# A causal latent-attention block with its query and key operands held as pairs of fp16 in place of pairs of rounded fp32

## The chip, the cores and the metric

The kernel runs on one core of a Trainium2 chip. A core has a matrix engine (TensorE, PE in the profile, with its weight loads as PEld), VectorE (DVE), ScalarE (ACT), GpSimd (POOL) and SyncE (SP), which mainly issues DMAs. The engines run side by side, each serves its own instructions in order, and they wait for one another by semaphores. TensorE writes to the accumulators in PSUM; ACT and DVE read them there. The metric is the time of one execution on the device in microseconds; lower is better.

## The reference

The input x has 2048 rows of 512 numbers, in fp32. One attention layer with compressed queries and keys is followed by a linear layer, each with a residual sum and a layer norm:

```python
cq = rms_norm(x @ w_qa.T, q_a_ln_w)                    # 2048 x 384
q = (cq @ w_qb.T).reshape(1, 2048, 16, 192)            # 16 heads: 128 plain + 64 rotary
ckv = x @ w_kva.T                                      # 2048 x (128 + 64)
ckv_l = rms_norm(ckv[..., :128], kv_a_ln_w)
k_nope, v = split((ckv_l @ w_kvb.T).reshape(1, 2048, 16, 256), 128)
# q_pe, k_pe: rotary parts; k_pe is one for all heads
scores = (q_nope @ k_nope.T + q_pe @ k_pe.T) * 192 ** -0.5, causal mask
out = softmax(scores) @ v, heads joined, @ w_o.T
x = layernorm(x + out)
x = layernorm(x + x @ (weight * scale_weight[:, None]).T + bias)
```

## The kernel before

**Numbers.** TensorE takes rounded fp32 (F32R) or fp16. To keep accuracy, an operand is held as a pair: a high part h, the value in the narrower type, and a low part l, the value less h. A product of two pairs takes three matmuls, hh, hl and lh. `split` (L61 to L68) makes a pair: one ACT instruction (L64, or L67 with a scale) writes h, one DVE instruction (L65 or L68) writes l. Before the change, softmax weights and values are pairs of fp16 (L495, L498; V), and the query latents, query weights, queries, keys and rotary parts are pairs of F32R.

**Heads.** The key up-projection is folded into the query weights: `weights_q` (L139) multiplies, for each of four groups of four heads, the plain query weights by the key weights (L170) and splits the result; so all heads share one key of 128 numbers, `Kn`, and one rotary key, `Kp`. In `score` (L409 to L427) a tile of scores takes five matmuls (L421): three with the plain query `qn` and `Kn`, two with `pe` and `Kp`. Of `pe`'s 128 partitions 64 hold the rotary query's high part and 64 its low part, while `Kp` holds the key twice. The causal mask is added on the diagonal tile, by a small matmul (L423) or by DVE (L427).

**Setup and side work.** x is worked through in eight half blocks of 256 rows. `project_x` (L198) computes keys for 128 rows at a time, with x stationary (L221), then the query latents already transposed, 3 x 12 matmuls of 256 columns with the weights stationary (L251). Keys are normalised with `rsqrt` on POOL (L195, L196), transposed by TensorE (L268, L269) and split. The latents are not normalised: `query_norms` computes 1/rms for each row (L283, L288) into `rq`, which enters as the scale of the softmax. Latents and weights that are not needed at once go to DRAM (`cq_d`, `wq_d`, `wpe_d`), and `load_block`, `load_wq`, `load_wpe` fetch them again for each query block. Half blocks 0 and 1 and weight group 0 come first, in setup; the rest is side work between the steps of query block 0.

**Query blocks.** Four blocks of 512 rows; in each, `units` (L627) goes through eight pairs of heads and four tiles of 128 rows. Per head and tile: scores, row maximum (DVE L459), exp with row sum (ACT L474; in block 0, L515 and L521), normalised weights as a pair (ACT L495, DVE L498), a transposing DMA on SP's queue, and the product with the values (`values`, L551), a few tiles later. `project_nope` (L391) and `project_pe` (L347) make the queries of the next pair between the score tiles; POOL forms `pe` (L359, L360, L373, L374). A score tile has its row of 128 queries against all keys up to the diagonal, cut into chunks of at most 512 columns (`chunks`, L35): 320 to 512 columns in block 1, up to four chunks in block 3.

**Order.** In setup and block 0 a scheduler orders each engine's instructions by a timeline of its own, with four PSUM buffers tagged `m` for all small products. From block 1 on TensorE's and SP's order is the program's, and from block 3 also that of ACT and DVE. In block 3 three PSUM buffers take turns for score tiles of up to 1024 columns, two of them for each head. After block 3 the output stage applies w_o and the linear layer with pairs of F32R (L770, L880).

## Time and profile before

| | us |
|---|---|
| median of 3 runs | 1588.42 (1587.66 to 1588.46) |
| profiled execution, its span | 1586.4 |
| setup, to the first score matmul | 36.66 |
| block 0 | 212.09 |
| block 1 | 242.85 |
| block 2 | 356.10 |
| block 3 | 476.80 |
| output stage | 261.90 |

The boundaries are the starts of the first score matmul of each block. In lines of groups, the name of the tile written stands left of the arrow, the tiles read right of it, then partitions x elements and the type, xcount, busy time and mean duration of one in ns, and the idle time of the engine just before them. In a line of the timeline the first number is the start, the second the time from the first start to the last end of the merged instructions. A matmul's duration includes filling and draining, which overlap with its neighbours', so that starts, not durations, tell its cost.

### The profile page before, as it was taken

The numbers are of one execution on the slowest core, as the hardware profiler recorded it, in microseconds if no ns is written. First come the engines' busy times: TensorE is split into PE (matmuls) and PEld (weight loads), VectorE is DVE, ScalarE is ACT, GpSimd is POOL, SyncE is SP. The second block draws the span as 40 slices with busy tenths as digits, with TensorE's granted clock in tenths as the row PEclk, the third lists the DMA queues.
The fourth block names the chain that finished last, engine by engine and source line by source line (L and its number), as shares of the span: only waits on it lengthen the run. The fifth ranks groups of instructions, "written<-read, shape, count | busy, mean of one in ns | idle before, by whom it ended". The sixth has DMA issues, their size and how long they took to land. (4 is left out here: it accounts for less than half of the span.)

```text
span 1586.4 us, 24671 instructions
## 1 busy us (share of the span) xinstructions
PE 1546.3 (97%) x9130; PEld 1291.1 (81%) x9130; DVE 1161.2 (73%) x2099; ACT 924.7 (58%) x1631; POOL 361.5 (23%) x434
## 2 busy tenths in 40 slices
PE   8899998999999999999999999999999999999997
PEld 7688877888887788888888788888888886788886
DVE  6777777878787978787786877877777775465564
ACT  5767776665665676666765665665666665311120
POOL 2243325154016204050032401400400000022132
PEclk9999999999999999999999999999999999999999
DMA  7879877788897987788897888878678798433230
GB/s 230 258 197 240 191 191 160 147 176 190 149 218 163 173 163 165 159 162 170 160 204 148 168 145 168 156 143 165 140 143 176 148 233 196 146 118 122 94 113 33
DMA packets 633032, 262.49 MB, mean 165 GB/s; under 512 B 570288, under 2 KB 611376, under 8 KB 631888
## 3 DMA queue, kind: packets, MB, share of 16 engines
q1 hardware_dynamic: 621472, 233.62, 68.8%
q0 software_dynamic: 4672, 17.73, 3.6%
q10 hardware_dynamic: 6768, 9.57, 2.1%
q8 instruction: 72, 1.18, 0.3%
q14 instruction: 48, 0.39, 0.1%
HBM read 83.17 MB, written 35.13 MB: 75 GB/s over the span
## 5 line engine op out<-in xcount | busy, mean ns | idle before, releaser
L421 PE MATMUL s<-Kn,qn 128*128 128x512 f32 (+4 forms) x1920 | 521.1, 376 | 9.4 <-ACT pr L474 4.4
L474 ACT ACTIVATE pr<-s,bias,rq 128x1024 f32<-128x1024 f32 (+3 forms) x320 | 324.4, 1017 | 217.0 <-DVE bias L468 157.2
L498 DVE SCALAR_TENSOR_TENSOR hl<-pr,inv,hl 128x1024 f16<-128x1024 f32 (+7 forms) x320 | 359.6, 1137 | 38.7 <-ACT hl L495 34.9
L421 PEld LDWEIGHTS s<-Kn,qn 128*128 128x128 f32 x1920 | 339.5, 190 | 55.7 <-ACT pr L474 7.4
L551 PEld LDWEIGHTS <-V 128*128 128x128 f16 x3264 | 302.5, 98 | 86.6 <-issue 47.6
L551 PE MATMUL o<-ring,V 128*128 128x256 f16 x3024 | 362.9, 273 | 2.5 <-DVE qn L68 1.2
L421 PE MATMUL s<-Kp,pe 128*128 128x512 f32 (+4 forms) x1280 | 361.4, 363 | 0.0
L495 ACT ACTIVATE hl<-pr,inv 128x1024 f16<-128x1024 f32 (+7 forms) x320 | 294.6, 961 | 91.3 <-issue 34.5
L459 DVE TENSOR_REDUCE neg<-s 128x1 f32<-128x1024 f32 (+3 forms) x320 | 317.8, 993 | 38.0 <-PE s L421 34.9
L421 PEld LDWEIGHTS s<-Kp,pe 128*128 128x128 f32 x1280 | 234.0, 189 | 29.6
L359 POOL TENSOR_TENSOR prod<-prod 128x512 f32<-128x512 f32 x15 | 19.4, 1292 | 639.1 <-DVE prod L352 639.0
L391 PE MATMUL ps_qn<-cq,wq 128*128 128x512 f32 x576 | 145.1, 397 | 3.1 <-ACT ot L556 1.7
L770 PE MATMUL acc<-wvo,oh 128*128 128x512 f32 x448 | 143.9, 402 | 1.8 <-ACT pr L474 1.8
L374 POOL TENSOR_TENSOR pe<-prod,ph 32x512 fp32r<-32x512 f32 x92 | 138.8, 1509 | 6.0
L391 PEld LDWEIGHTS ps_qn<-cq,wq 128*128 128x128 f32 x576 | 107.3, 190 | 24.8 <-ACT ot L556 2.4
L770 PEld LDWEIGHTS acc<-wvo,oh 128*128 128x128 f32 x448 | 83.1, 188 | 23.2 <-issue 3.8
L486 DVE TENSOR_SCALAR inv<-sums 128x1 f32<-128x1 f32 x128 | 27.0, 211 | 97.5 <-ACT pr L474 97.5
L770 PE MATMUL acc<-wvo,ol 128*128 128x512 f32 x224 | 88.1, 393 | 0.0
L556 ACT ACTIVATE ot<-o 128x256 f32<-128x256 f32 x128 | 48.4, 378 | 45.2 <-PE o L551 39.6
L347 PE MATMUL ps_pe<-cq,wpe 128*128 128x512 f32 x288 | 73.8, 402 | 0.2 <-DMA cq<-cq_d 0.2
L64 ACT ACTIVATE oh<-o 128x1024 fp32r<-128x1024 f32 x28 | 29.7, 1060 | 65.6 <-PE acc L770 50.0
L65 DVE TENSOR_TENSOR ol<-o,oh 128x1024 fp32r<-128x1024 f32 x28 | 38.8, 1387 | 39.3 <-ACT oh L64 39.3
(147 smaller groups left out, 1631.6 us busy)
## 6 DMA issues: line engine op xcount, KB each, us to landing
wq<-wq_d SPq DMA_DIRECT2D x22, 768.0 KB, 5.7
o<-ot_d SPq DMA_DIRECT2D x32, 512.0 KB, 3.3
ot_d<-ot SPq DMA_DIRECT2D x97, 128.0 KB, 2.4
wpe<-wpe_d SPq DMA_DIRECT2D x10, 768.0 KB, 5.4
wq<-wq_d POOLq DMA_DIRECT2D x9, 768.0 KB, 6.4
cq_d<-cqst SPq DMA_DIRECT2D x18, 256.0 KB, 4.8
wo<-in_wo_dram SPq DMA_DIRECT2D x4, 1024.0 KB, 5.3
x<-in_x_dram SPq DMA_DIRECT2D x16, 256.0 KB, 3.7
```

Source lines behind the costliest of these rows:

```text
L65: nc.vector.tensor_tensor(l, ps, h.bitcast(F32), ALU.subtract)
L347: nc.tensor.matmul(ps, w[:, i, lt, x * P : (x + 1) * P], cq[:, k, lt, :], start=n == 0, stop=n == 8)
L374: (nc.gpsimd if not quick or (b, g) == (0, 0) and j % 2 else nc.vector).tensor_tensor(pe[64 + 32 * x : 96 + 32 * x, j, :], rp[q, x, :], ph ...
L391: nc.tensor.matmul(ps, w[:, i, lt, j * P : (j + 1) * P], cq[:, k, lt, :], start=n == 0, stop=n == 8)
L421: nc.tensor.matmul(ps[:, :w], lhs, K[:, i, c0 : c0 + w], start=n == 0, stop=n == 4)
L459: nc.vector.tensor_reduce(neg[:, ti : ti + 1], v, axis=AX.XY, op=ALU.max, negate=True)
L474: nc.scalar.activation(pr[:, c0 : c0 + n * w].rearrange("p (a c) -> p a c", a=n), v, AF.Exp, bias=bias, scale=r, accum_out=sums[:, ti : ti ...
L495: nc.scalar.activation(hl[:, 0, c], pr[:, c], AF.Copy, scale=inv)
L498: nc.vector.scalar_tensor_tensor(hl[:, 1, c], pr[:, c], inv, hl[:, 0, c], ALU.mult, ALU.subtract)
L551: nc.tensor.matmul(ps[:, :256], vt[:, i, k % 4, :], v[:, :, l, k, :], start=n == 0, stop=n == 3 * kts - 1)
L556: nc.scalar.activation(ot, ps[:, :256], AF.Copy)
L770: nc.tensor.matmul(acc, l[:, t, c], state["wvo"][p][:, i, j, :], start=p == 0 and j == 0 and n == 0, stop=p == NPAIR - 1 and j == 1 and n ...
```

## The change

Query latents, query weights, plain queries and plain keys become pairs of fp16. `split16` makes them, always with a scale, since fp16 has a narrow range. The scales come from norms computed on chip: `weights_q` first forms the sum of squares of a whole group (ACT Square with a running sum, a matmul with ones, a DVE sum, a root on POOL) and splits its products, now copied to SBUF, only then; `first_scales` takes a norm of `kvln` in setup. The latents are now normalised before they are stored: `project_x` computes 128 rows at a time with x stationary (12 matmuls of 384 columns), squares and scales them, transposes them by TensorE and splits them. The score scale is then one number for a group of heads (`er`) instead of one for a row.

The rotary parts stay F32R in block 0, with a key tile of its own (`Kp0`), and are fp16 from block 1 on. The scale of the rotary key needs all 2048 rows: `project_x` keeps it in fp32 (`Kr`) with sums of squares, and behind the last half block `late_keys` forms the scales and splits it into `Kp`. From block 1 on the rotary tables `cs` are multiplied on POOL by one of those scales when they are loaded.

Tiles, loads and stores of these operands have half the bytes; the two halves of a weight group lie apart in DRAM. The instructions of TensorE for fp16 are a weight load and a matmul each, for F32R one that does both. Input layout and output stage are unchanged.

```diff
+K_UP = 1024.0
+C_UP = 1024.0
+W_TOP = 32768.0
+C_TOP = 20100.0
+TINY = 1.0e-30
...
+    def split16(src, h, l, scale):
+
+        nc.scalar.activation(h, src, AF.Copy, scale=scale)
+        nc.vector.scalar_tensor_tensor(l, src, scale, h, ALU.mult, ALU.subtract)
...
-    cq_d = [dram.tile([P, 2, LT, QB], F32R, name=f"cq_d{b}") for b in range(NB)]
-    wq_d = [dram.tile([P, 2, LT, 512], F32R, name=f"wq_d{g}") for g in range(4)]
-    wpe_d = [dram.tile([P, 2, LT, 256], F32R, name=f"wpe_d{g}") for g in range(4)]
+    cq_d = [dram.tile([P, 2, LT, QB], F16, name=f"cq_d{b}") for b in range(NB)]
+    wq_d = [dram.tile([P, 2, 2, LT, 256], F16, name=f"wq_d{g}") for g in range(4)]
+    wpe_d = [dram.tile([P, 2, LT, 256], F16, name=f"wpe_d{g}") for g in range(4)]
...
+    def root(dst, src, n=1):
+
+        t = small.tile([P, 4], F32, tag="rs", name="rt_t")
+        nc.gpsimd.tensor_scalar_add(t[:, :n], src, TINY)
+        nc.gpsimd.tensor_tensor(dst, t[:, :n], half, ALU.pow)
...
+    def column_total(dst, sums, n):
+
+        ps = psum["m"].tile([P, 512], F32, tag="m", name="ps_tot")
+        nc.tensor.matmul(ps[:, :n], ones, sums, start=True, stop=True)
+        nc.vector.tensor_reduce(dst, ps[:, :n], axis=AX.X, op=ALU.add)
...
+        tot = small.tile([P, 1], F32, tag="tot", name="tot")
+        column_total(tot, sq, 1)
+        root(kvn, tot)
+        nc.vector.tensor_scalar(kvn, kvn, C_TOP, None, ALU.mult)
+        k0 = small.tile([P, 1], F32, tag="k0", name="k0")
+        nc.vector.reciprocal(k0, kvn)
+        nc.vector.tensor_scalar(kvq[0], kvln, k0, None, ALU.mult)
+        nc.vector.tensor_scalar(ku, k0, K_UP, None, ALU.mult)
...
+        column_total(tot, ksum, S // P)
+        fk = small.tile([P, 1], F32, tag="fk", name="fk")
+        root(fk, tot)
+        z = small.tile([P, 1], F32, tag="z", name="z")
+        nc.vector.scalar_tensor_tensor(z, fk, K_UP, kvn, ALU.mult, ALU.add)
+        k1 = small.tile([P, 1], F32, tag="k0", name="k1")
+        nc.vector.reciprocal(k1, z)
+        nc.vector.tensor_scalar(kvq[1], kvln, k1, None, ALU.mult)
+        nc.vector.tensor_scalar(up, k1, fk, K_UP / W_TOP, ALU.mult, ALU.mult)
+        nc.vector.tensor_scalar(er[1], fg, z, SM_SCALE / (W_TOP * C_UP * K_UP), ALU.mult, ALU.mult)
+        nc.vector.reciprocal(ks, fk)
+        nc.vector.tensor_scalar(ks, ks, W_TOP, None, ALU.mult)
...
     def weights_q(g, direct=None):
...
-            split(raw, to[:, 0], to[:, 1], sc)
-            move(nc.sync, wpe_d[g][:, :, lt], to)
+            nc.scalar.activation(
+                junk[:, :256], rpe[:, lt], AF.Square, scale=sc, accum_out=sums[:, LT + lt : LT + lt + 1]
+            )
+        wr = pa.tile([P, LT, 512], F32, tag="wr", name=f"wr{g}")
...
             ps = psum["m"].tile([P, 512], F32, tag="m", name=f"ps_wq{g}_{lt}")
             for j in range(4):
                 nc.tensor.matmul(ps[:, j * P : (j + 1) * P], raw[:, j, :], wk[:, j, :], start=True, stop=True)
+            nc.scalar.activation(junk, ps, AF.Square, scale=sc, accum_out=sums[:, lt : lt + 1])
+            nc.vector.tensor_copy(wr[:, lt], ps)
+            if lt < LT - 1:
+                yield
+        tot = small.tile([P, 1], F32, tag="tot", name="tot")
+        column_total(tot, sums, 2 * LT)
+        root(fg[:, g : g + 1], tot)
+        nc.vector.tensor_scalar(
+            er[0][:, g : g + 1], fg[:, g : g + 1], kvn, SM_SCALE / (W_TOP * C_UP * K_UP), ALU.mult, ALU.mult
+        )
+        rf = small.tile([P, 1], F32, tag="rf", name="rf")
+        nc.vector.reciprocal(rf, fg[:, g : g + 1])
+        qa = small.tile([P, LT], F32, tag="qa", name="qa", bufs=2)
+        nc.vector.tensor_scalar(qa, qln, rf, W_TOP, ALU.mult, ALU.mult)
+        st = Kp.rearrange("p a c -> p (a c)")[:, : 4 * LT * 256].rearrange("p (b a l c) -> p b a l c", b=2, a=2, l=LT)
+        to = direct[0] if direct is not None else st[:, 0]
+        for lt in range(LT):
+            sc = qa[:, lt : lt + 1]
+                split16(
+                    wr[:, lt].rearrange("p (a c) -> p a c", a=2), st[:, :, 0, lt], st[:, :, 1, lt], sc
+                )
             else:
...
+                split16(wr[:, lt, :256], to[:, 0, lt], to[:, 1, lt], sc)
+        pt = direct[1] if direct is not None else pa.tile([P, 2, LT, 256], F16, tag="wpst", name=f"wpst{g}")
+        for lt in range(LT):
+            split16(rpe[:, lt], pt[:, 0, lt], pt[:, 1, lt], qa[:, lt : lt + 1])
...
+            nc.sync.dma_start(wq_d[g], st)
+        nc.sync.dma_start(wpe_d[g], pt)
+        yield
...
     def project_x(hb, wkv, wqa, direct=None, raws=None):
...
+            nc.scalar.activation(junk[:, :P], ps[:, :P], AF.Square, scale=P ** -0.5, accum_out=ms[:, 0:1])
...
+            nc.scalar.activation(
+                junk[:, :64], kp[:, 0, :], AF.Square, accum_out=ksum[:, 2 * hb + i : 2 * hb + i + 1]
+            )
+            pc = psum["m"].tile([P, 512], F32, tag="m", name=f"ps_cq{hb}_{i}")
+            n = 0
+            for kt in range(KT):
+                for x_, w_ in ((xh, wqa[0]), (xh, wqa[1]), (xl, wqa[0])):
+                    nc.tensor.matmul(pc[:, : LT * P], x_[:, kt, cols], w_[:, kt, :], start=n == 0, stop=n == 11)
+                    n += 1
+            nc.scalar.activation(
+                junk[:, : LT * P], pc[:, : LT * P], AF.Square, scale=(LT * P) ** -0.5, accum_out=ms[:, 1:2]
+            )
+            rk = small.tile([P, 2], F32, tag="rk", name="rk")
+            rsqrt(rk, ms, 2, 1e-6)
+            nk = pa2.tile([P, P], F32, tag="nk", name="nk")
+            nc.vector.tensor_scalar(nk, ps[:, :P], rk[:, 0:1], None, ALU.mult)
+            nq = pa2.tile([P, LT * P], F32, tag="nq", name="nq")
+            nc.scalar.activation(nq, pc[:, : LT * P], AF.Copy, scale=rk[:, 1:2])
...
-            if i:
-                query_norms()
...
-            nc.scalar.activation(sq, ps[:, :256], AF.Square, scale=(LT * P) ** -0.5)
-            if lt:
-                nc.vector.tensor_tensor(acc, acc, sq, ALU.add)
...
+            pq = psum["m"].tile([P, LT, P], F32, tag="m", name=f"ps_qt{hb}_{i}")
+            for lt in range(LT):
+                nc.tensor.transpose(pq[:, lt, :], nq[:, lt * P : (lt + 1) * P], ident)
+            to = slice(o + i * P, o + (i + 1) * P) if direct is not None else cols
+            split16(pq, st[:, 0, :, to], st[:, 1, :, to], C_UP)
             yield
-        norms.append((hb, acc))
...
+        split16(pt[:, 0].rearrange("p a c -> p (a c)"), Kn[:, 0, cols], Kn[:, 1, cols], K_UP)
+        kf = pt[:, 1].rearrange("p a c -> p (a c)")
+        nc.scalar.activation(Kr[:, cols], kf, AF.Copy)
+        if hb < 2:
+            split(kf, Kp0[:, 0, cols], Kp0[:, 1, cols], ku)
+            nc.sync.dma_start(cq_d[b][:, :, :, half_of], st)
...
+    def late_keys():
+        late_scales()
+        yield
+        for c in range(0, S, 512):
+            split16(Kr[:, c : c + 512], Kp[:, 0, c : c + 512], Kp[:, 1, c : c + 512], ks)
+            yield
...
     def load_block(b):
...
-        cq = prj.tile([P, 2, LT, QB], F32R, tag="cq", name=f"cq{b}")
+        cq = prj.tile([P, 2, LT, QB], F16, tag="cq", name=f"cq{b}")
         if b:
-            move(state["queue"], cq, cq_d[b])
+            state["queue"].dma_start(cq, cq_d[b])
         cs = prj.tile([P, 2, QB], F32, tag="cs", name=f"cs{b}")
         (state["queue"] if b else nc.sync).dma_start(cs, a["csq"][b])
+        if b:
+            nc.gpsimd.tensor_scalar(cs, cs, up, None, ALU.mult)
...
+        w = state["wq", b, p] = prj.tile([P, 2, LT, 256], F16, tag="wq", name=f"wq{b}_{p}")
+        state["queue"].dma_start(w, wq_d[p // 2][:, p % 2])
...
+        w = state["wpe", b, g] = prj.tile([P, 2, LT, 256], F16, tag="wpe", name=f"wpe{b}_{g}")
+        state["queue"].dma_start(w, wpe_d[g])
...
+        kind = F16 if b else F32R
+        ph = prj.tile([P, 2, QB], kind, tag="ph", name=f"ph{b}_{g}")
         nc.scalar.activation(ph, rp, AF.Copy)
-        pe = blk.tile([P, 4, QB], F32R, tag="pe", name=f"pe{b}_{g}")
+        pe = blk.tile([P, 4, QB], kind, tag="pe", name=f"pe{b}_{g}")
...
+        qn = blk.tile([P, 2, 2, QB], F16, tag="qn", name=f"qn{b}_{p}")
...
-            split(ps, qn[:, 0, j, :], qn[:, 1, j, :], kvln)
+            split16(ps, qn[:, 0, j, :], qn[:, 1, j, :], kvq[1 if b else 0])
...
-        ops = [(qh, Kn, 0), (qh, Kn, 1), (ql, Kn, 0), (qp, Kp, 0), (qp, Kp, 1)]
+        kp = Kp if b else Kp0
+        ops = [(qh, Kn, 0), (qh, Kn, 1), (ql, Kn, 0), (qp, kp, 0), (qp, kp, 1)]
         n = 0
         for lhs, K, i in ops:
             nc.tensor.matmul(ps[:, :w], lhs, K[:, i, c0 : c0 + w], start=n == 0, stop=n == 4)
...
     def head_scores(pools, b, p, j, qt, nk, prev):
-        t = 4 * b + qt
-        r = rq[:, t : t + 1]
+        r = er[1][:, p // 2 : p // 2 + 1]
```

## Prediction

> **What bounds the kernel now.** I read the page first, then the busy time by stage, then the groups by form, then the timeline of TensorE, then the waits. The page says who is busy.
>
> ```profile
> span 1586.4 us, 24671 instructions
> PE 1546.3 (97%) x9130; PEld 1291.1 (81%) x9130; DVE 1161.2 (73%) x2099; ACT 924.7 (58%) x1631; POOL 361.5 (23%) x434
> ```
>
> The median of the runs is 1588.42 us, 2.0 above this execution's span; I add that 2.0 to every sum. The smallest change that a measurement of this kernel can tell from none is about 0.2%, 3.2 us.
>
> The windows cut the span at the first score matmul of each query block: setup, blocks 0 to 3, output stage. Columns: stretch, its length, busy time of PE, PEld, DVE, ACT, POOL, then granted clock, DMA share, GB/s.
>
> ```profile
> 0.00:36.66 36.66, 32.45 (x206) 27.30 (x207) 21.84 (x55) 20.88 (x54) 10.96 (x30) 1.00 0.69 224
> 36.66:248.75 212.09, 197.78 (x1309) 170.18 (x1308) 160.01 (x374) 153.30 (x392) 69.69 (x123) 0.98 0.85 216
> 248.75:491.60 242.85, 238.66 (x1432) 202.23 (x1429) 197.06 (x416) 151.51 (x242) 82.73 (x74) 0.99 0.85 175
> 491.60:847.70 356.10, 353.45 (x2149) 298.10 (x2149) 291.52 (x546) 240.15 (x432) 83.16 (x72) 1.00 0.84 167
> 847.70:1324.50 476.80, 473.54 (x2893) 393.08 (x2891) 355.70 (x511) 301.91 (x442) 65.10 (x56) 1.00 0.80 158
> ```
>
> Blocks 1 to 3 are TensorE from end to end; DVE is next, at 75 to 82%. In their 1075.8 us TensorE's listed waits sum to 10 us. So there a cheaper matmul is a shorter kernel. What a matmul costs is not its duration (pipelined, they overlap) but the distance between starts:
>
> ```profile
> 1299.25 2.13 PE L551 MATMUL o<-ring,V 128*128 128x256 f16 x18
> 1301.13 0.94 PE L421 MATMUL s<-Kn,qn 128*128 128x512 f32 x3
> 1301.91 0.63 PE L421 MATMUL s<-Kp,pe 128*128 128x512 f32 x2
> 1302.38 0.86 PE L421 MATMUL s<-Kn,qn 128*128 128x512 f32 x3
> ...
> 1303.55 0.77 PE L421 MATMUL s<-Kn,qn 128*128 128x448 f32 x3
> ```
>
> Five fp32 matmuls of 512 columns fill 1302.38 to 1303.55: 234 ns each. Over the trace the median distances at L421 are 234, 201, 176, 147, 118 ns for 512, 448, 384, 320, 256 columns, 230 at L391, 228 at L347. The fp16 ones of 256 columns (L551; above, 17 distances in 2.13 us less the last one's 0.27) stand 109 apart. The only fp16 matmuls of 512 columns are the ten warm-ups, whose closest starts are 216 apart. 109 and 216 give 0.418 ns a column plus 2, so fp16 should cost 216, 189, 162.5, 136, 109: from 9 ns (256) to 18 ns (512) less.
>
> **What the change takes from TensorE.** Block 1 has 160 score matmuls of each of 320, 384, 448, 512 columns, 144 of L391, 72 of L347: 160 x (11 + 13.5 + 12 + 18) + 144 x 14 + 72 x 12 = 11.6 us. Block 2: 80 x 9 + 320 x 13.5 + 560 x 18 + 144 x 14 + 72 x 12 = 18.0. Block 3: 160 x 36.5 + 800 x 18 + 126 x 14 + 54 x 12 = 22.6. Together **52.2 us**. Setup and block 0 have 162 of L391, 90 of L347 and three of five score matmuls (rotary pairs stay fp32 there): 3.4 + 96 x 9 + 48 x 13.5 + 48 x 18, together 5.7.
>
> The order of TensorE's instructions in blocks 1 to 3 is unchanged, and of ACT's and DVE's nearly so. What follows close behind: DVE's 197, 291.5 and 355.7 us stand in stretches of some 231, 338 and 454, which is 85, 86 and 78%. The tightest wait is in block 3, where the second score tile of a head reuses the buffer that an exp (L474) frees: in the trace that exp ended 0.88 us before (median), in 10 of 63 cases under 0.6; a head's first tile gets 0.15 to 0.18 us shorter. I charge **+3** for waits that appear, bounds 0 and +26 (half of the gain). The halved loads of weights and latents (768 KB in 5.7 us, 22 on SP) are hidden, and stay so; their cover is a pair's work of over 30 us.
>
> POOL's splits of the rotary part (1.29 us each, cast 0.76) now read and write fp16, which no row shows: from 0 to twice as long, 36 us for a group instead of 18. A group's users start over 40 us later, so nothing; without that cover up to 18 us a group, 11 groups. Block loads gain a POOL multiplication of the tables, 128x1024, by a row of 1.29 us for 128x512 some 2.6 us; SP issues the loads far ahead in blocks 2 and 3. In block 1 it stands before the latents' load in POOL's queue and waits for the new scales; users come some 11 us later, about what it all takes. Nothing, up to +5.
>
> **Setup: new round trips.** Now each 128 rows of latents are normalised before the transpose, and TensorE's order puts the three transposes right behind the twelve matmuls that they depend on, in setup with nothing between. One trip: Square 128x384 from PSUM 0.52 (row of 128x384, L64), accumulator read 0.19, POOL add 0.23 and pow 0.76 (128x2 rows of L195, L196), scaling on ACT 0.52, three hand-offs of 0.1: 2.5 us. Four trips: **+10.0**. On ACT the next half's split (2 x 0.63) stands ahead of the first Square and 0.5 ahead of the last scaling: **+1.7**. The weights now wait for their norm:
>
> ```profile
> 24.91 3.07 PE L170 MATMUL ps_wq<-wk,wqb_r 128*128 128x128 f32 x24
> 27.81 0.50 PE L283 MATMUL ps_rq<-ones,acc 128*128 128x1 f32 x4
> ```
>
> Today L391 starts at 28.42, 0.6 us behind L170. Then ACT has about 3.4 us of splits and Squares left (three of 0.69 + 0.19, four smaller of some 0.4, one in progress), and the chain total, sum, add and pow, three small DVE steps, first split adds 0.25 + 0.3 + 1.0 + 0.7 + 0.5, together 6.2 (I take 6.3): **+5.7**. So long an idle time also slows what follows, as one of today shows:
>
> ```profile
> 43.68 1.13 PE L170 MATMUL ps_wq<-wk,wqb 128*128 128x128 f32 x8 [4.10 <-DMA wqb<-in_wqb_dram]
> 44.57 5.95 PE L391 MATMUL ps_qn<-cq,wq 128*128 128x512 f32 x18
> ```
>
> The same 18 matmuls took 4.33 us from 28.42 on, 1.6 less. The windows around the waits show the clock (columns as above):
>
> ```profile
> 42.00:49.50 7.50, 5.82 (x23) 4.86 (x24) 4.24 (x6) 7.35 (x13) 1.88 (x3) 0.77 1.04 387
> 62.50:69.50 7.00, 4.62 (x24) 3.81 (x23) 5.15 (x17) 6.22 (x16) 0.00 (x0) 0.76 0.97 265
> 130.00:138.00 8.00, 6.04 (x27) 4.86 (x26) 5.72 (x14) 6.16 (x19) 1.08 (x2) 0.79 1.11 342
> 245.00:255.00 10.00, 5.93 (x26) 5.10 (x25) 8.84 (x14) 5.48 (x11) 2.29 (x4) 0.74 0.56 156
> ```
>
> They hold TensorE's waits of 4.10, 2.38, 1.96 and 2.68 us, and behind each the clock was halved for 3.4 us (6.8 behind the last); behind waits up to 1.75 us it was not. The new wait for the norm is one more: **+1.6**. The trips of 2.5 us stand among the rows that slow: 4 x 1.6 = **+6.4**, bound 0. The Trainium skill, in "TensorE: Matmul & The Clock Gate", section "What's actually happening", names at least one idle window of about 3.4 us as what halves the clock. By it trips of 2.5 us would cost nothing further, and the sum would be 1564; the rows of 1.96 to 2.68 us disagree, and I go by them.
>
> Projection itself: 24 x 176 + 6 x 109 for 36 x 120 ns per half block, +0.55; eight times +4.4, less 32 norm matmuls of about 0.1, −3.2: **+1.2** in all.
>
> **Block 0.** Three more transposes have under 0.5 us of other work ahead of them in TensorE's order: 2.0 + 2.0 + 2.5 = **+6.5**. Whether these halve the clock depends on what stands around them; half of 3 x 1.6, **+2.4**, bounds 0 and 4.8. ACT gains, per half block, two Squares for keys (0.25 + 0.19), two 128x384 Squares and scalings for six passes over 128x256 less: some 1.9; per weight group Squares of 3 x (0.69 + 0.5 + 0.38) = 4.7; four splits of late keys, 2.6. In block 0: 6 x 1.9 + 3 x 4.7 + 2.6 = 28 us. From 52 us on ACT is busy 142 of 197 us, and would be 170, 86%. DVE loses about what it gains. Beside TensorE this is hidden while 27 us remain; I charge **+4**, bounds 0 and +28.
>
> **Sum.** −52.2 − 5.7 + 3 + 10.0 + 1.7 + 5.7 + 1.6 + 6.4 + 1.2 + 6.5 + 2.4 + 4 = −15.4, on 1586.4 + 2.0: 1573 us.
>
> **Rivals.** (1) The round trips are covered and slow no clock: without 10.0 + 1.7 + 6.4 + 6.5 + 2.4 + 4 = 31, 1542. For: in blocks 1 to 3 TensorE hides as long chains; against: in its new order nothing stands between. (2) **Slower**: DVE and the exp chain swallow half of the matmul gain: 26 in place of 3, 1596. For: 0.88 us of slack and DVE at 86%; against: its 14% idle. It decides when the exps end later than a tile is needed in most of the 63 cases, not in 10. (3) Slower, ACT becomes the limit of block 0: its queue is served in order, and each of the 12 scalings there also waits about 1.1 us for POOL behind its Square: 28 + 13 = 41 us in place of 6.5 + 2.4 + 4, 1601. ACT's 142 + 41 = 183 us must pass the 197 of the stretch for it; 14 us are missing. (4) The change does not do what it says: fp16 of 512 columns stands as far apart as fp32, since only warm-ups show 216. Then 1520 x 18 + 576 x 14 + 288 x 12 ns, 39 us, are lost: 1612. Against: the 109 for 256 columns leaves 2 ns over the column rate.
>
> **How the numbers follow.** My sum 0.66 (1556 to 1588), rival 1 0.10, rival 2 0.08, rival 3 0.07, rival 4 0.03, others 0.06. Faster by over 0.2% is below 1585.2: 0.63 of my sum, 0.10, and 0.03 of the others, 0.76. Within 0.2%: 0.03 and 0.03, 0.06. Slower: 0.18 for the rivals 2 to 4. The range from 1546 to 1595 leaves out 0.13 of the slower cases and most of rival 1.
>
> **What would show it.** Starts of fp16 512-column scores 216 apart, and blocks 1 to 3 1023 to 1030 us long: right. The first score at 56 to 64 us instead of 36.66, with TensorE waiting for ACT ahead of each transpose in setup, and the clock there under 1.00. Block 0 from 207 to 225 us. Wrong: a distance of over 225, waits for the exps of over 10 us in blocks 1 to 3, or ACT busy over 95% of block 0.

## The result, and the profile after

The changed kernel takes 1605.09 us (median of 4 runs, 1599.94 to 1606.74), the kernel before 1588.44 beside it: a ratio of 1.0097, 95% interval 1.0079 to 1.0115. It is slower by 1%, and outside the predicted range. The head of the page of the changed kernel:

```profile
span 1605.0 us, 24447 instructions
PE 1507.0 (94%) x9062; PEld 1013.6 (63%) x9062; DVE 1158.3 (72%) x2108; ACT 956.4 (60%) x1733; POOL 353.9 (22%) x425
```

TensorE is busy 39 us less in a span 19 us longer. The windows of the changed kernel (same cuts and columns as before: setup, then blocks 0 to 3) show where:

```profile
0.00:61.90 61.90, 44.12 (x191) 32.88 (x192) 26.33 (x65) 31.43 (x87) 10.76 (x28) 0.81 0.42 145
61.90:313.42 251.52, 200.26 (x1258) 147.14 (x1256) 165.11 (x375) 174.44 (x461) 68.95 (x114) 0.90 0.50 126
313.42:539.94 226.52, 223.70 (x1431) 140.13 (x1429) 192.86 (x414) 151.00 (x241) 80.52 (x75) 0.99 0.75 164
539.94:876.60 336.66, 334.67 (x2148) 210.16 (x2148) 287.00 (x543) 240.45 (x432) 82.18 (x74) 1.00 0.70 160
876.60:1341.60 465.00, 452.17 (x2894) 282.71 (x2892) 351.89 (x514) 301.94 (x444) 60.30 (x54) 1.00 0.71 156
```

Setup +25.2, **block 0 +39.4**, blocks 1 to 3 −16.3, −19.4 and −11.8, output stage +1.5. In block 0 TensorE stands idle for 251.5 − 200.3 = 51.3 us, before for 14.3. The fp16 matmuls do what was expected of them; in the timeline of TensorE, five of 512 columns start between 1312.16 and 1313.24, 216 ns apart:

```profile
1312.16 0.81 PE L493 MATMUL s<-Kn,qn 128*128 128x512 f16 x3
1312.81 0.59 PE L493 MATMUL s<-Kp,pe 128*128 128x512 f16 x2
1313.24 0.73 PE L493 MATMUL s<-Kn,qn 128*128 128x448 f16 x3
```

TensorE's waits in block 0 (us in total, times, longest):

```profile
PE ps_qt L334 <- ACT nq L325: 22.8, 4, 7.8
PE ps_pe L417 <- DMA wpe<-wpe_d: 9.0, 1, 9.0
PE s L493 <- ACT pr L591: 8.0, 6, 2.7
PE s L493 <- DVE pe L445: 5.6, 1, 5.6
PE o L621 <- ACT ot L626: 4.6, 1, 4.6
```

In the first row three of the four waits, 7.5, 7.8 and 6.4 us, are of latent transposes that stand nearly directly behind their projection in TensorE's order. One of them, in the timelines of ScalarE and TensorE:

```profile
109.89 2.55 ACT L442 ACTIVATE pe<-prod 32x512 fp32r<-32x512 f32 x4 [0.30 <-POOL prod L429]
112.47 1.06 ACT L433 ACTIVATE ph<-prod 128x1024 fp32r<-128x1024 f32 x1
113.55 1.27 ACT L442 ACTIVATE pe<-prod 32x512 fp32r<-32x512 f32 x2
...
114.83 1.26 ACT L442 ACTIVATE pe<-prod 32x512 fp32r<-32x512 f32 x2
...
116.50 0.49 ACT L317 ACTIVATE junk<-ps_cq 128x384 bf16<-128x384 f32 x1
...
119.06 0.58 ACT L325 ACTIVATE nq<-ps_cq,rk 128x384 f32<-128x384 f32 x1 [0.71 <-POOL rk L271]
```

```profile
111.11 1.05 PE L221 MATMUL ps_wq<-wk,wqb 128*128 128x128 f32 x8
119.69 0.90 PE L334 MATMUL ps_qt<-ident,nq 128*128 128x128 f32 x3 [7.53 <-ACT nq L325]
```

The projection was done by 111.3, and the matmuls on `ps_wq` that TensorE had in between by 112.2. The projection's Square (L317) could start only at 116.50, since ScalarE, which takes its instructions in order, had a group's rotary copies in front of it (109.89 to 116.1). The scaling and the transposes followed 3.2 us later. From 114.4 on, within the wait, the clock is halved for 10.2 us, with TensorE at work for 4.9 of them, nearly all behind the wait (two windows, cut at 114.4; the clock is the third number from the end):

```profile
106.00:114.40 8.40, 6.16 (x41) 5.15 (x38) 6.34 (x11) 6.66 (x13) 4.04 (x5) 1.00 0.43 118
114.40:124.60 10.20, 4.91 (x19) 3.05 (x20) 6.35 (x11) 6.61 (x19) 2.38 (x3) 0.50 0.10 33
```

### The profile page after: what moved, and what is told of

It reads as the page before. It is cut to its first block, busy times and chain, and to the rows that moved or that the text cites. A ratio compares the mean times of both kernels' runs of the same rounds, so it can differ in the third digit from the quotient of the medians.

```text
span 1605.0 us, 24447 instructions
## 1 busy us (share of the span) xinstructions
PE 1507.0 (94%) x9062; PEld 1013.6 (63%) x9062; DVE 1158.3 (72%) x2108; ACT 956.4 (60%) x1733; POOL 353.9 (22%) x425
## 5 line engine op out<-in xcount | busy, mean ns | idle before, releaser
L493 PE MATMUL s<-Kn,qn 128*128 128x512 f16 (+4 forms) x1920 | 469.5, 350 | 23.1 <-ACT pr L545 14.5
L545 ACT ACTIVATE pr<-s,bias,er 128x1024 f32<-128x1024 f32 (+3 forms) x320 | 324.0, 1015 | 208.9 <-DVE bias L539 162.7
L493 PE MATMUL s<-Kp,pe 128*128 128x512 f16 (+6 forms) x1280 | 353.2, 358 | 5.6 <-DVE pe L445 5.6
L493 PEld LDWEIGHTS <-qn 128*128 128x128 f16 x1920 | 185.1, 98 | 174.9 <-issue 36.5
L493 PEld LDWEIGHTS <-pe 128*128 128x128 f16 x1152 | 113.0, 98 | 103.3 <-issue 0.3
L462 PE MATMUL ps_qn<-cq,wq 128*128 128x512 f16 x576 | 141.1, 393 | 5.6 <-ACT wq L68 2.5
L445 POOL TENSOR_TENSOR pe<-prod,ph 32x512 f16<-32x512 f32 (+1 forms) x92 | 127.7, 1388 | 14.7 <-issue 8.8
L462 PEld LDWEIGHTS <-wq 128*128 128x128 f16 x576 | 58.1, 102 | 71.0 <-issue 11.3
L417 PE MATMUL ps_pe<-cq,wpe 128*128 128x512 f16 x288 | 69.3, 387 | 9.1 <-DMA wpe<-wpe_d 9.0
L444 POOL CAST pe<-prod 32x512 f16<-32x512 f32 x88 | 67.2, 763 | 3.3
```

Of the source, the lines that this page charges most:

```text
L417: nc.tensor.matmul(ps, w[:, i, lt, x * P : (x + 1) * P], cq[:, k, lt, :], start=n == 0, stop=n == 8)
L444: nc.gpsimd.tensor_copy(to, rp[q, x, :])
L445: (nc.gpsimd if not quick or (b, g) == (0, 0) and j % 2 else nc.vector).tensor_tensor(pe[64 + 32 * x : 96 + 32 * x, j, :], rp[q, x, :], ph ...
L462: nc.tensor.matmul(ps, w[:, i, lt, j * P : (j + 1) * P], cq[:, k, lt, :], start=n == 0, stop=n == 8)
L493: nc.tensor.matmul(ps[:, :w], lhs, K[:, i, c0 : c0 + w], start=n == 0, stop=n == 4)
L545: nc.scalar.activation(pr[:, c0 : c0 + n * w].rearrange("p (a c) -> p a c", a=n), v, AF.Exp, bias=bias, scale=r, accum_out=sums[:, ti : ti ...
```

## The experiments

All are compared with the kernel before on the same chip (1589.2 to 1590.1 us there). The table gives each one's setup and block 0 from its profile. "Idle" is the length of block 0 less TensorE's busy time in it; "lost" is half of TensorE's busy time in the stretches with the clock at half, from the trace's clock records. What is left, work at full clock, is 192.7 us before and 182.7 to 186.7 in all the others. Setup and block 0 are those of one execution, while the median is of 4 to 10 runs. Block 0 is the same code, in the same order on TensorE, in the changed kernel and in e6, and took 251.5 and 256.2 us: a difference of some 5 us in this column is not told from scatter. TensorE's order in block 0 is the changed kernel's also in e5, and nearly in e2 and e10, and e7 keeps e3's; in the other runs the scheduler made a new one, so that they show an edit together with its new order.

| kernel | median us | ratio to before, 95% | setup | block 0 | idle | lost |
|---|---|---|---|---|---|---|
| before | 1588.44 | 1 | 36.7 | 212.1 | 14.3 | 5.1 |
| changed | 1605.09 | 1.0097, 1.0079 to 1.0115 | 61.9 | 251.5 | 51.3 | 15.2 |
| e1 late transposes | 1587.44 | 0.9988, 0.9975 to 1.0000 | 56.6 | 238.6 | 38.6 | 14.4 |
| e2 copies on VectorE | 1601.06 | 1.0071, 1.0055 to 1.0086 | 63.3 | 245.6 | 47.5 | 12.1 |
| e3 no latent norms | 1584.14 | 0.9966, 0.9956 to 0.9976 | 50.8 | 232.1 | 39.7 | 7.1 |
| e4 no weight norms | 1588.76 | 1.0003, 0.9986 to 1.0020 | 60.6 | 237.7 | 44.1 | 10.8 |
| e5 rotary weights direct | 1601.73 | 1.0071, 1.0051 to 1.0091 | 62.2 | 244.4 | 44.7 | 14.7 |
| e6 no row maximum in block 3 | 1586.65 | 0.9983, 0.9973 to 0.9993 | 57.7 | 256.2 | 56.6 | 14.6 |
| e7 = e3 + e5 | 1575.62 | 0.9909, 0.9885 to 0.9934 | 48.6 | 226.4 | 32.8 | 8.4 |
| e8 = e7 + e4 | 1554.15 | 0.9781, 0.9764 to 0.9798 | 43.2 | 208.4 | 21.2 | 4.3 |
| e9 = e1 + PSUM freed early | 1587.25 | 0.9981, 0.9963 to 0.9999 | 55.4 | 238.8 | 40.1 | 12.6 |
| e10 filled waits in setup | 1605.33 | 1.0095, 1.0075 to 1.0114 | 58.6 | 252.1 | 52.6 | 13.7 |
| e11 = e9 + e5 + filled waits | 1583.27 | 0.9958, 0.9942 to 0.9973 | 55.1 | 236.5 | 38.2 | 13.1 |
| e12 = e8 + Squares | 1556.43 | 0.9788, 0.9764 to 0.9812 | 45.7 | 209.4 | 22.9 | 2.6 |
| e13 = e8, copies on GpSimd | 1564.43 | 0.9845, 0.9826 to 0.9865 | 43.1 | 224.0 | 30.4 | 10.9 |
| e14 = e11, copies on GpSimd | 1590.73 | 1.0005, 0.9996 to 1.0015 | 53.4 | 240.8 | 43.6 | 10.4 |
| e15 = e11, weights as in e12 | 1567.51 | 0.9851, 0.9834 to 0.9869 | 51.1 | 222.8 | 30.9 | 7.9 |

**e1: the transposes a step later.**

```diff
             yield
-            pq = psum["m"].tile([P, LT, P], F32, tag="m", name=f"ps_qt{hb}_{i}")
...
-            split16(pq, st[:, 0, :, to], st[:, 1, :, to], C_UP)
-            yield
+            turns.append((i, nq))
+            if i:
+                turn(*turns.pop(0))   # the same transposes and split, for part 0
+                yield
...
+        yield                         # behind the key transposes
+        turn(*turns.pop(0))
```

> Same work as the changed kernel; only the program order differs: the three transposes of a 128-row part of the latents are given a step later (behind the next part's matmuls, the second part's behind the key transposes). In TensorE's order of block 0 the work between a part's last projection matmul and its transposes was 4.3, 4.7, 0.1, 3.5, 2.9, 5.3, 0.1, 3.5, 3.7, 2.1, 0.0, 3.5 us; here it is 6.9 to 13.7 us but for two parts of hb 2 (7.6 and 2.7). Theory A (transposes placed right behind their matmuls, while ScalarE, served in order, still has the rotary copies in front of the Square and of the scaling): the three waits of 7.5, 7.8 and 6.4 us and the half clock behind them (27 us at half speed, so up to 13) go: block 0 from 251.5 to 215 to 228 us; in the setup two of four round trips are covered in part, 61.9 to about 55; in all about 1565 to 1580 us. Rival B (ScalarE's load is the limit of block 0): its work is the same, the waits turn up at other lines, block 0 stays above 245 us and the whole above 1595 us.

It lies between the two: 1587.44 us, block 0 at 238.6, 12.9 us shorter. TensorE's waits there (lines are this kernel's own, L334 is now the scaling):

```profile
PE ps_cq L324 <- ACT nq L334: 9.1, 2, 6.1
PE o L630 <- ACT ot L635: 7.2, 2, 4.7
...
PE o L630 <- ACT nq L334: 5.4, 1, 5.4
```

The transposes hardly wait any more (1.4 us, once), but the next projection and a value product do, for the PSUM tile that the scaling still holds.

**e2: block 0's rotary copies on VectorE.**

```diff
-                if quick:
+                if b == 0:
+                    nc.vector.tensor_copy(to, rp[q, x, :])
+                elif quick:
                     nc.scalar.activation(to, rp[q, x, :], AF.Copy)
```

> The changed kernel with the 32-partition copies of block 0's rotary parts (32 of 0.64 us, 20 us) on VectorE in place of ScalarE; TensorE's order is the changed kernel's. Theory A: the three long waits on the scaled latents shrink from 7.5, 7.8 and 6.4 us to 2.5 to 4 us each (the Square no longer stands behind copies), block 0 shrinks by 8 to 16 us, and the transposes still wait; in all 1589 to 1597 us. Rival B (ScalarE's load is the limit): block 0 shrinks by the 20 us of work that leaves it, 1585 us or less. Rival D (the round trip itself, GpSimd's power and the semaphores, not the copies, makes the long waits): they stay above 6 us and the time stays within 3 us of 1605.

With TensorE's order nearly unchanged the waits on the scaled latents shrink as theory A has it:

```profile
PE ps_pe L417 <- DMA wpe<-wpe_d: 12.6, 1, 12.6
PE s L495 <- ACT pr L593: 10.9, 8, 2.7
PE ps_qt L334 <- ACT nq L325: 10.1, 4, 3.4
```

So the copies in front did make 2.8-us trips into waits of 6 to 8 us, and theory D falls. But other waits grew, block 0 gained 5.9 us only, less than theory A's 8 to 16 and rival B's 20, and the whole is 1601.06 us.

**e3: the latents without their norm.** The projection is that of before, its tile split at a fixed factor; left out is the scaling of the fp16 latents by their norm.

```diff
-            nc.scalar.activation(nq, pc[:, : LT * P], AF.Copy, scale=rk[:, 1:2])
...
-                nc.tensor.transpose(pq[:, lt, :], nq[:, lt * P : (lt + 1) * P], ident)
+                split16(ps[:, :256], st[:, 0], st[:, 1], C_UP)
...
-        r = er[1][:, p // 2 : p // 2 + 1]
+        r = rr[:, p // 2, 4 * b + qt : 4 * b + qt + 1]   # er times the row's norm
```

> The changed kernel with its latents undone: projected transposed as before (weights stationary), split into fp16 at a fixed factor of 1024 without their norm, the norm in the exponential's scale per row as before. No round trip and no bare transposes of latents; the weights' norm, the fp16 pairs and all else stay. Theory A: setup 61.9 to about 42 to 46 us, block 0 251.5 to 205 to 212 us, blocks 1 to 3 unchanged at 1028 us within 3; in all 1540 to 1552 us. Rival B (ScalarE's load, the Squares of the weights and the fp16 copies, is the limit of block 0): its work falls from 174 us by 12 Squares and 12 scalings of 0.5 us only, block 0 stays above 235 us, in all above 1570 us.

Both theories miss: 1584.14 us. The trips are gone, and block 0 is 19.4 us shorter, not 40 to 46; 39.7 us of idle time remain. The wait for the rotary weights (8.9) is still there, and one of 9.0 us for a transposed probability tile has come at the block's end.

**e4: the weights without their norm.**

```diff
-        column_total(tot, sums, 2 * LT)
-        root(fg[:, g : g + 1], tot)
+        nc.vector.memset(fg[:, g : g + 1], W_TOP / 1024.0)
...
-            nc.scalar.activation(junk, ps, AF.Square, scale=sc, accum_out=sums[:, lt : lt + 1])
```

> The changed kernel with the query weights scaled by a fixed 1024 in place of their norm: left out are the Squares on ScalarE (24 of about 0.5 to 0.7 us, 18 of them in block 0), the column total on TensorE and the power on GpSimd; the round trips of the latents stay. Theory A: the setup loses the wait for the weights' norm, 61.9 to about 54 to 57 us; block 0's long waits stay (they come from the latents), 245 to 252 us; in all 1592 to 1600 us. Rival B (ScalarE's load is the limit of block 0): 11 us more go in block 0, in all 1583 to 1589 us.

1588.76 us and 237.7 in block 0: the number of rival B. Yet what ScalarE causes did not shrink: the waits on the scaled latents are 25.8 us in 3. Gone are the waits for the rotary weights' load and for the first rotary split. So two readings stayed open, load or hold, until e12.

**e5: block 0's rotary weights without the way through DRAM.**

```diff
-        pt = direct[1] if direct is not None else pa.tile([P, 2, LT, 256], F16, tag="wpst", name=f"wpst{g}")
+        pt = direct[1] if direct is not None else prj.tile([P, 2, LT, 256], F16, tag="wpe", name=f"wpe0_{g}")
+        state["wpe", 0, g] = pt
```

> The changed kernel with the scaled rotary weights of groups 1 to 3 split straight into the tile that block 0's rotary projection reads; before, they went by DRAM (a store from the staging tile, then a load). TensorE's order is the changed kernel's. Theory E (the weights' norm holds all splits of a group back to its end, so that the store and the load of the rotary weights fall due at once: the wait of 9.0 us at 169 to 178 us of the span, half clock behind it): that wait goes, block 0 from 251.5 to 238 to 243 us, in all 1591 to 1597 us. Rival F (the DMA rings were full there, with three transposes of 13.7 us and the loads of x; the next transfer in line is late by as much): the wait turns up at another line, block 0 stays above 248 us.

The wait goes, and of the others only that of the value products grows, from 4.6 to 7.3 us. Block 0 loses 7.1 us (244.4), a little less than theory E had; the whole is 1601.73, above its range of 1591 to 1597, and a gain of 3.4 us that is not clear of noise. In the changed kernel the load stood so (issues from 140 to 180 us; the last number is the median time to landing):

```profile
xr<-in_xT_dram ACTq DMA_DIRECT2D x3, 256.0 KB, 11.3
...
wpe_d<-wpst SPq DMA_DIRECT2D x1, 384.0 KB, 3.1
...
wpe<-wpe_d POOLq DMA_DIRECT2D x1, 384.0 KB, 15.8
...
PT<-hl SPq DMA_TRANSPOSE x6, 7.0
```

It was issued at 162.39, 3.7 us behind its store, and TensorE needed it at 169.24. The other loads of this tile on GpSimd's queue took 3.6 to 4.4 us; at that this one, too, would have come in time. So the wait took both, a load issued late and a slow one. The transfers issued beside it were slow as well, loads of x with 15.6 and 11.3 us and three transposes with 10.8 to 17.3; which of them made it so is not shown. In e4, without the hold of the weights' norm, the load for this projection was issued 58 us ahead of its use. In e6 it took 19.4 us and the wait 13.7, which is the 4.7 us by which block 0 is longer there.

**e6: no row maximum in block 3.**

```diff
+        if b == 3:
+            bias = zero
-            nc.vector.tensor_reduce(neg[:, ti : ti + 1], v, axis=AX.XY, op=ALU.max, negate=True)
+            if b < 3:
+                nc.vector.tensor_reduce(neg[:, ti : ti + 1], v, axis=AX.XY, op=ALU.max, negate=True)
```

> The changed kernel with no row maximum in block 3: its reductions on VectorE and the bias are left out, the exponential takes a bias of zero and so starts as soon as its own scores stand. Theory G (block 3 gains 11.8 us of the 22.6 that its matmuls gain, because the chain scores, maximum, bias, exponential now ends when TensorE wants the PSUM tile back): block 3 falls from 465 to 453 to 458 us, blocks 1 and 2 stay within 1 us, in all 1592 to 1598 us. Rival H (TensorE's own work is what is left in block 3): it stays within 2 us of 465.

TensorE's waits in block 3, the changed kernel first, then this one:

```profile
PE s L493 <- ACT pr L545: 12.7, 13, 2.1
```

```profile
PE s L495 <- ACT pr L550: 0.8, 1, 0.8
```

From its first to its last score start block 3 falls from 463.2 to 445.8 us, more than theory G's range; rival H falls. The whole is 1586.65. Of the 17.4 us, 12 are these waits; TensorE is also busy 5.3 us less (452.2 to 446.9), which stays open. The edit takes 141 us of work off VectorE in block 3 as well, so that the length of the chain and VectorE's load are not told apart.

**e7 and e8: the mends together.** e7 is e3 with e5's edit, e8 adds e4's.

> e3_no_trip (latents projected transposed, a fixed factor, norm in the exponential's scale) with the direct rotary weights of e5. Its block 0 was 232.1 us: 185.3 of work at full clock, 39.7 idle, 7.1 lost at half clock. Theory E: the wait of 8.9 us on the load goes, block 0 to 217 to 224 us; in all 1568 to 1577 us. Rival F: another transfer is late in its place, above 1580 us.

> e7 with the query weights scaled by a fixed 1024 in place of their norm (left out: the Squares of the weights, the column total and the power): fp16 pairs without any norm on the way to the first scores. Setup 50.8 us in e3; the waits for the weights' norm there were 2.6 and 0.9 us, and ScalarE loses six Squares: 44 to 48 us. Block 0: ScalarE loses 11 us of work, 210 to 220 us. In all 1553 to 1567 us, faster than both kernels. If the schedule opens other waits in block 0, as in e3 (9.0 us on a transposed tile at its end), up to 1575 us.

e7: 1575.62 us, block 0 at 226.4, 2 us over its range. e8: 1554.15 us, 2.2% under the kernel before and 51 us under the changed one, every number inside or under its range. Its setup and block 0:

```profile
0.00:43.20 43.20, 34.89 (x217) 25.73 (x218) 29.45 (x90) 24.09 (x67) 11.60 (x30) 1.00 0.59 202
43.20:251.57 208.37, 187.17 (x1305) 140.27 (x1302) 169.98 (x394) 156.73 (x420) 69.69 (x117) 0.97 0.64 152
```

It is the fastest version; its fixed factors fit these weights and latents, which the norms did for any. Setup and block 0 are 61.9 us shorter than in the changed kernel; blocks 1 to 3 gave part of that back, 1041.0 us in this profile against 1028.2, with 16.8 us of waits for the exponentials in block 3. Why these grew stays open.

**e9: PSUM freed at once.**

```diff
+            nc.vector.tensor_copy(nk, ps[:, :P])
+            nc.vector.tensor_copy(nq, pc[:, : LT * P])
...
-            nc.scalar.activation(nq, pc[:, : LT * P], AF.Copy, scale=rk[:, 1:2])
+            nc.scalar.activation(nq, nq, AF.Copy, scale=rk[:, 1:2])
```

> e1_late_turn, and VectorE copies the raw latents and keys out of PSUM as soon as they stand (8 copies more of each kind in all, about 0.5 and 0.3 us), so that the projection's PSUM tiles do not wait for the norm and for ScalarE's scaling. Theory A2 (in e1 the trips only changed their line: TensorE waited 9.1 us at the next projection for the PSUM tile that the scaling frees, 6.1 in one place): these waits go, block 0 from e1's 238.6 to 225 to 232 us; in all 1577 to 1584 us. Rival B (ScalarE's queue as a whole is late, whoever waits for it): the waits move on to outputs and exponentials, block 0 stays above 235 us, in all above 1584 us.

Theory A2 falls: 1587.25 us, block 0 at 238.8. The projection no longer waits for the scaling, but now value products wait 6.9 us for VectorE's new copy, and the rotary weights' load 9.8. Its numbers are those of rival B.

**e10: the setup's trips filled with matmuls on zeros.**

```diff
+            if direct is not None:
+                for _ in range(14):
+                    nc.tensor.matmul(pq.rearrange("p l c -> p (l c)"), ramp[:, :P], ramp[:, : LT * P], start=True, stop=True)
             for lt in range(LT):
                 nc.tensor.transpose(pq[:, lt, :], nq[:, lt * P : (lt + 1) * P], ident)
```

> The changed kernel with 14 matmuls on zeros of 384 columns (fp16, 2.3 us) in front of the three transposes of each of the setup's four trips, in the PSUM tile that the transposes then fill, and TensorE's order in that part written out; they do no part of the result. Theory C (behind a wait of 2.5 to 2.8 us the clock is halved, and that costs the setup as much as the waits: 22.7 us busy at half clock, 11.3 lost): TensorE is busy in the trips, no half clock until the weights' norm, the first score at 50 to 55 us in place of 61.9; in all 1592 to 1599 us. Rival C2 (the clock in the setup is low for another reason, the start of the program): the first score stays at 59 to 64 us.

Windows over the four trips, the changed kernel first:

```profile
15.00:49.60 34.60, 22.49 (x118) 21.14 (x117) 11.38 (x26) 17.33 (x55) 5.60 (x14) 0.80 0.24 81
```

```profile
15.00:48.00 33.00, 27.49 (x179) 21.60 (x178) 13.50 (x33) 19.75 (x63) 6.44 (x16) 0.97 0.30 96
```

The clock holds in the trips (0.97 for 0.80), and the weights' total comes at 45.1 in place of 49.5. But behind the wait for the weights' norm it is then halved for 6.8 us, not 3.4; the first score comes at 58.6, short of theory C's 50 to 55, and the time of the whole stays at 1605.33. With the setup's code unchanged, e6 had its first score at 57.7, so the gain is not told from scatter.

**e11: all norms kept, with the mends.** It is e9 with e5's edit, and matmuls on zeros in the setup's waits.

> All norms of the changed kernel kept, with three mends together: the order and the early PSUM release of e9, the direct rotary weights of e5, and matmuls on zeros in the setup's waits as in e10 (12 before the first transposes, 10 before the keys'). If the effects add: setup 56.6 to about 50, block 0 e9's less 6: in all 1563 to 1576 us, under the kernel before by 0.8 to 1.6%. If the schedule opens other waits in block 0, up to 1585 us.

1583.27 us, faster than the kernel before by 0.4%, but the effects did not add: block 0 is 236.5 us, and its idle time 38.2, as in e1 and e9. The waits only changed their lines.

**e12: the Squares without the hold.** Between e7 and e8 two things differ: ScalarE's Squares, and the splits that wait for the norm. This one puts the Squares back and leaves their sums unused.

```diff
 # against e8
...
+            nc.scalar.activation(junk, ps, AF.Square, scale=sc, accum_out=sums[:, lt : lt + 1])
 # against e7
-        column_total(tot, sums, 2 * LT)
-        root(fg[:, g : g + 1], tot)
+        nc.vector.memset(fg[:, g : g + 1], W_TOP / 1024.0)
```

> e8_fixed_scales with the weights' Squares on ScalarE put back (24 of 0.5 to 0.7 us, 18 of them in block 0, about 11 us there), their sums unused: no total, no power, no split that waits for them. It parts the two things in which e7 (block 0 226.4 us) and e8 (208.4) differ. Load theory B (each microsecond on ScalarE's queue in block 0 is paid for): block 0 back to 217 to 222 us, in all 1563 to 1570 us. Hold theory E (the splits of a group wait for the norm at its end and then come all at once): block 0 stays at 206 to 212 us, in all 1552 to 1559 us.

Block 0 of e7, then of e12:

```profile
48.62:275.00 226.38, 193.62 (x1318) 143.96 (x1316) 175.19 (x409) 168.38 (x451) 73.35 (x123) 0.94 0.61 138
```

```profile
45.73:255.12 209.39, 186.46 (x1296) 139.09 (x1294) 169.45 (x391) 166.29 (x448) 68.76 (x117) 0.98 0.60 151
```

ScalarE works nearly as long in both (168.4 and 166.3 us), and block 0 is 17.0 us shorter; by the medians the whole is 19.2 us shorter, 1556.43. The load theory falls. The hold theory is borne out, with one rival left: the edit also gave TensorE a new order in block 0, and no run takes the hold away and keeps the order.

**e13 and e14: the copies of groups 1 to 3 on GpSimd**, in e8 and in e11.

```diff
-                if quick:
+                if quick and (b, g) in ((0, 0), (1, 0)):
                     nc.scalar.activation(to, rp[q, x, :], AF.Copy)
```

> e8_fixed_scales with block 0's rotary copies of groups 1 to 3 (24 of 0.64 us, 15 us) on GpSimd in place of ScalarE; GpSimd takes about 0.76 us for one in the later blocks. Theory B: block 0 from 208.4 to 198 to 204 us, in all 1544 to 1551 us. If ScalarE's queue is no longer on the path once the norms are gone: within 3 us of 1554; GpSimd's six extra microseconds in a row may hold the loads in its queue, up to 1560 us.

> e11_all_norms with the same 24 rotary copies on GpSimd. In e1, e9 and e11 the waits only changed their line: block 0's idle time stayed at 38.6, 40.1 and 38.1 us. Theory B (ScalarE's queue, not the trips' place, is what is late in block 0): idle falls by about 15 us, block 0 from 236.5 to 218 to 226 us, in all 1565 to 1573 us. Theory A (the trips themselves): GpSimd also does the trips' power and now does it behind the copies, block 0 stays above 232 us, in all above 1579 us.

Both became slower, by 10 and 7 us, with 13 and 14 us less on ScalarE in block 0. In e13 value products now wait for VectorE's query splits:

```profile
PE o L637 <- DVE qn L69: 16.1, 3, 7.0
```

VectorE was slowed there: of its 28 subtractions for block 0's `pe`, the 13 that ran beside a GpSimd copy took 1.00 us each (median), against 0.68 in e8, where no such copy runs on GpSimd. That this alone made VectorE late is not shown, and the order changed too. No run made block 0 shorter in step with the load taken off ScalarE.

**e15: the latents' norms alone.** e11 with e12's edit to the weights.

> e11_all_norms (latents' norms kept, transposes a step later, PSUM released early, rotary weights direct, the setup's waits filled) with the query weights scaled by a fixed 1024 and their Squares left on ScalarE, unused, as in e12. So it differs from e11 by the weights' hold alone and from e12 by the latents' norms alone. If the hold was worth the 17 us that e7 and e12 differ by in block 0 whatever else is done, block 0 falls from e11's 236.5 to 217 to 223 us, and in all 1558 to 1566 us. If the transposes, given later, also cover the trips once the hold is gone: block 0 at 208 to 214 us as in e12, in all 1550 to 1557 us. If the trips cost the same wherever the transposes stand: above 226 us and above 1568 us.

Block 0 is 222.8 us, as the first theory said; 1567.51 us, 1.5 over its range. So the hold, with the new order that its end brings, is worth 17.0 us of block 0 without the latents' norms (e7 to e12) and 13.7 with them (e11 to e15), and the latents' norms, their transposes given late, 13.4 (e12 to e15). By the medians of the whole kernel these are 19.2, 15.8 and 11.1 us.

## Why the prediction was wrong

**Right: the matmuls.** The distances 216, 189, 162, 136 and 109 ns are those forecast. Blocks 1 to 3 took 1028.2 us, within the 1023 to 1030 named, a gain of 47.6 for 49.2. The parts differ: work at full clock fell by 13.2, 18.8 and 23.1 us in the three blocks (11.6, 18.0 and 22.6 forecast), 55.1 in all for 52.2. In block 3 the term of +3 for new waits was mis-sized: idle time went from 3.3 to 12.8 us. That the sum came so near is partly luck, two errors of opposite sign. The waits for the exponentials passed the 10 us named as the sign of error, by the mechanism of rival 2 (e6), in one block only.

**Right: the setup in sum.** +25.2 us, against terms adding up to 25.4 before the projection's small ones. The four trips waited 10.8 us (10.0 charged). The clock behind them was halved for 13.6 us, and 6.5 were lost (6.4 charged). But that part is chance: in e6 the same trips halved it once. The rest is partly luck: the weights' norm set 4.2 us between the last matmul on the weights and the next projection (+5.7 charged), and 3.2 us were lost at half clock from 8.6 to 15.4, which no term priced.

**Wrong: block 0.** Forecast were +6.5, +2.4 and +4 less fp16's gain there; it took +39.4: 36.9 of idle time and 10.0 of lost clock, less 7.6 of work at full clock. Three terms failed.

- *The three transposes behind their matmuls, 2.0 + 2.0 + 2.5.* Three were forecast, and three waited, 7.5, 7.8 and 6.4 us (a fourth 1.1). Each was charged a setup trip, with ScalarE free. The prediction listed ScalarE's queue as a rival by its load, but did not price what stands in that queue at these three places: some 6 us of rotary copies. e2 shows it: without them no wait is over 3.4 us.
- *The weights' norm in block 0.* It was charged in the setup (+5.7) and not again for the groups split in block 0. There the splits come all at once behind the norm, then a store, then a load issued 7 us before its use, which took 15.8 us to land: 9.0 us of wait (e5: block 0 7.1 us shorter). "The halved loads are hidden" held in blocks 1 to 3; in block 0 one load of rotary weights came too late. The wait of 5.6 us for the first rotary split is in e7 and gone in e12 as well. In all, 17.0 us went with the hold (e7 to e12), though with a new order on TensorE.
- *The clock, +2.4.* The time at half clock in block 0 rose from 10.2 to 48.8 us, and the lost time from 5.1 to 15.2, +10.0.

In steps of one edit, block 0 goes from 251.5 to 244.4 (rotary weights direct), 226.4 (latents split without their norms), 209.4 (weights' hold gone) and 208.4 (Squares gone, a step within the scatter), against 212.1 before.

**Rival 3** gave 1601 us, near the result, by the wrong mechanism: ScalarE as the limit of block 0 by its load. It is busy 174 of 251.5 us, 69%; 10 us of Squares there cost 1 (e8, e12), and taking copies off it saved 5.9 us for 20 (e2) or nothing (e13, e14, with a new order). It matters by its order, as the engine on which the trips wait.

**Open.** In e1, e9 and e11 the idle time of block 0 stayed at 38 to 40 us whatever wait was mended; e15 shows that the hold kept 7 of it there and the latents' norms 8 (to e12's 22.9), but not through which chain each wait moved on. The setup of e8, with neither the latents' nor the weights' norm ahead of a split, is still 6.5 us longer than before; why stays open.

## What to carry to other kernels

A dependence costs what stands ahead of it in each queue that it crosses, at its own place: price a new round trip by the timeline of the in-order engine there, not by the same trip where that engine is free. A scale that needs the whole of a tensor holds back every step that uses it and makes them fall due together, stores and reloads among them; here a cheap reduction went with 17 us of block 0, where its Squares on ScalarE went with 1 (e7, e12, e8). Mending one wait at a time may only move it; take the dependence away once to see what it is worth.

## What was not expected of the hardware

Whether a short wait halves TensorE's clock was partly chance here: its length did not settle it. The four trips of the setup wait 2.47, 2.77, 2.77 and 2.75 us, by the same code, in the changed kernel and in e6: the clock was halved behind all four in the one and behind the first alone in the other. The first scores stood 4 us apart, part of it from a half stretch of 6.8 us at the start, of 3.4 in e6. Counted over all 17 profiled executions are the waits of TensorE that begin at full clock, 12 us or more into the span, with no other wait above 1 us in the 4 us ahead; a wait counts as followed by a half stretch if one begins between its start and 3.5 us behind its end. The clock was halved behind 18 of 146 waits of 1.0 to 2.0 us, 41 of 71 of 2.0 to 2.5, 26 of 35 of 2.5 to 3.0, 9 of 10 of 3.0 to 3.5, and all 64 that were longer. The half stretches last 3.41 us or multiples of it.

The Trainium skill, "TensorE: Matmul & The Clock Gate", section "What's actually happening", names a free-running window of 3413 ns, which agrees with the stretches and with the chance; its threshold of a whole idle window does not, since waits of 2.0 to 3.0 us, which can't fill one, halved the clock behind 67 of 106.
